# A convolution-attention and edge-branch network: 2 by 2 blocks in place of 4 by 1 columns, larger value patches, and a second layout of x

## The chip, the cores and the metric

The kernel runs on one core of a Trainium2 chip. The metric is the device time of the whole program in microseconds. Matmuls run on TensorE (PE in the profile, its weight loads PEld), elementwise work on VectorE (DVE) and ScalarE (ACT), some on GpSimd (POOL). SyncE (SP) issues nearly all DMAs; ScalarE issues those that rearrange strips and store edge features.

## The reference

The input x is (4, 512, 64, 64) in float32: four images of 512 channels. Everything is float32. The first layer is a linear attention over 64 heads of 8 channels, twice: once on q, k, v, once on their 5 by 5 depthwise and grouped pointwise convolutions.

```
q, k, v = x @ wq.T, x @ wk.T, x @ wv.T                  # over channels
pw = grouped_1x1(depthwise_5x5(concat(q, k, v)))        # 8 channels a group
f = concat(qkv, pw), in heads of 24 channels: query, key, value
query, key = relu(query), relu(key)
scores = concat(value, ones) @ key.T                    # 9 x 8 per head, over the 4096 pixels
out = scores @ query;  out = out[:8] / (out[8] + 1e-15)
y = batchnorm(proj_1x1(out)) + x
```

The second layer makes four edge maps of y (Sobel, Laplace, diagonal, gradient), multiplies each by a 128 by 512 matrix, applies batchnorm and GELU, weights the 512 results by a channel attention of their means, mixes them by a 512 by 512 matrix, normalises over channels, applies GELU and adds y.

## The kernel before

**Groups.** Each image b is cut in 4 groups of 16 heads; one `Group` object per (b, g), 16 in all. A group projects keys and values (`keys_and_values`, 8 strips of 512 pixels), then queries (`queries`). The steps of a group that use the convolved queries (`convolve(QUERY, ...)`, the second half of `correlate`, `conv_*`) are run inside the next group's `keys_and_values`. `run` and `advance` interleave the steps of the groups with the stages of the image before: `project_out`, `edge_branches`, `fuse_out`, by shares of time written out by hand (`T_CONV`, `SHARE_Y` and so on). The order of TensorE is the program's; the other engines follow the program too, each in order, and SP's DMA queue is one of them. The first image has no stage beside it. After the last group, the last image's three stages run with wider tiles (side "left"), interleaved by `fill`.

**Strips.** A strip is a half image (32 rows) and one of four row phases: rows k, k+4, k+8, ... of 64 pixels. x lies in DRAM in this order. `project` multiplies it and copies the result to `strip`; four DMAs issued by ScalarE put it into `inps[t]`, where partition = (head of four, channel, row phase), and the rows are blocks of four.

**Convolution.** `convolve` (L402) computes the depthwise and the pointwise convolution at once: for each of 5 column shifts `DXS` and 2 row blocks, a 32 by 32 matrix `mat` for each of 16 tiles of the array, 512 columns at most, summed in four PSUM banks: 160 matmuls. `load_mat` builds `mat` by one GpSimd product of the two kernels. ScalarE evicts the banks with a ReLU (L415 for keys, in the order that `correlate` needs; L421 for queries).

**Correlation.** The convolved values are never formed. `values` (L290) projects values with pixels on partitions; four DMAs a strip (L303) store them in `near`, a padded copy of the image in DRAM, split in two halves of 8 heads. `load_near` (L442) loads patches of 4 rows by 8 pixels a partition, one load for each (half, jp, b) in four DMAs: jp picks the heads, b the upper or lower row block; `vals` has 3 such buffers of 8448 bytes a partition. `correlate` (L457) multiplies transposed convolved keys by these patches, 160 columns a matmul, in two PSUM banks for each jp. `weigh` (L475, L476) multiplies by the value kernel and sums.

**Output.** `divide` and `conv_divide` write the normalised queries of the 16 heads to DRAM (`heads`, `cheads`). `project_out` loads 8 tiles of 512 pixels a strip, multiplies by the folded projection (L661), adds shift and x (L666, VectorE), and writes rows of y four apart. For the last image 16 blocks run first, since the first edge rows need all four phases of a half; then edge steps alternate with filling (`FILL_*`).

**Fusion.** `fuse_out` (L850) loads four `ef` tiles a piece (8 buffers), squares into `sq` (3 buffers) and normalises. `late` marks the last two images.

Of the kernel before, what the change touches and what calls it, by code (L numbers as in the profile page):

```python
# [8 lines left out]
F32 = mybir.dt.float32  # L9
# [35 lines left out]


NB = H // 4 + 1
# [5 lines left out]
DXS = (0, -2, -1, 1, 2)  # L53
VROW = 4 * 66
# [19 lines left out]
FILL_EACH = (16 * FILL_Y + 40 * FILL_F - FILL_FIRST - FILL_ATT) / (4 * NJ // 2 - 1)  # L74
# [3 lines left out]
T_PROJ, T_TURN, T_SCORES, T_CONV, T_CORR, T_SMALL = 3.4, 0.5, 0.3, 10.6, 1.1, 0.9  # L78


WORK, VALS = 18, 3
# [8 lines left out]
def conv_seq_kernel(  # L90
    ctx: ExitStack, tc, x, wqkv, dpk, wtab, proj, projc, pwk, bn0, consts, vec, watt1, batt1, watt2, wbr, wfuse, out
# [26 lines left out]
    def squares(ap):  # L118

        return ap.rearrange("p (b x n) -> p n x b", b=4, n=4)  # L120
# [25 lines left out]
    for t in (KEY, QUERY):  # L146
        inps[t] = keep.tile([P, 4, NB, W], F32, name=f"inp{t}")
        nc.gpsimd.memset(inps[t][:, :, 0, :], 0.0)
        nc.gpsimd.memset(inps[t][:, :, NB - 1, :], 0.0)
# [7 lines left out]
    near = [dram.tile([2, NB, W + 4, 4, 66], F32, name=f"near{n}", bufs=1) for n in range(2)]  # L157
# [3 lines left out]
    def near_border(v):  # L161

        zeros = vals.tile([P, 8 * VROW], F32, name="zeros", tag="vals")
        nc.gpsimd.memset(zeros, 0.0)
        cols = v.rearrange("a b x r d -> (a b) x (r d)")
        for at in (0, W + 2):
            nc.sync.dma_start(out=cols[:, at : at + 2, :], in_=zeros[0 : 2 * NB, 0 : 2 * VROW])
        for b, r in ((0, 0), (NB - 1, 2)):
            nc.sync.dma_start(
                out=v[:, b, :, r : r + 2, :].rearrange("a x r d -> x a (r d)"),  # L170
                in_=zeros[0 : W + 4, 0:264],
            )
# [53 lines left out]
    class Group:  # L226


        def __init__(self, b, heads, cheads, folded, g):
# [3 lines left out]
            self.strip, self.rq, self.held, self.conv, self.near = {}, {}, {}, {}, {}  # L233
            self.nears = iter([(half, jp, b) for half in range(2) for jp in range(2) for b in range(2)])
# [7 lines left out]
        def load_mat(self, t):  # L242

            dp = gw.tile([P, 4, 48], F32, name="dp_sb", tag="dp_sb", bufs=2)
            nc.sync.dma_start(out=dp, in_=dpk[self.g, t // QUERY])
            self.mat[t] = gw.tile([P, 4, 40, 8], F32, name="mat", tag="mat")
            nc.gpsimd.tensor_tensor(  # L247
                self.mat[t],
                dp[:, :, 0:40].unsqueeze(3).to_broadcast([P, 4, 40, 8]),
                dp[:, :, 40:48].unsqueeze(2).to_broadcast([P, 4, 40, 8]),  # L250
# [11 lines left out]
        def project(self, t, j):  # L262
# [12 lines left out]

            r, b = (k + 2) % 4, 8 * half + (k + 2) // 4
# [5 lines left out]
            for n in range(4):  # L282
                nc.scalar.dma_start(out=inps[t][r::4, n, b : b + 8, :], in_=rows(s)[32 * n : 32 * n + 32, :, :])

        def values(self, j):
# [14 lines left out]
            b = 8 * half + (k + 2) // 4  # L300
            for a in range(2):
                for jp in range(2):
                    nc.sync.dma_start(  # L303
                        out=self.near_dram[jp, b + a : b + a + 7 : 2, 2 : W + 2, (k + 2) % 4, :].rearrange(
                            "c x d -> x c d"
                        ),
                        in_=vt[64 * a : 64 * a + 64, :, 2 * jp : 2 * jp + 2, :].rearrange("p c q d -> p c (q d)"),
                    )
# [75 lines left out]
        def divide(self, half):  # L384
            banks = self.spread_out(self.rec)
            for k in range(4):
                j = 4 * half + k
                q = work_tile("q")
                nc.vector.tensor_mul(q, self.rq.pop(j), banks[k])
                nc.sync.dma_start(out=self.heads[j, :, self.g, :], in_=q)  # L390
# [3 lines left out]
        def convolve(self, t, half):  # L394
            banks = quad_tiles("cv")
            last = len(DXS) * 2 - 1
            for n, (dx, b) in enumerate((dx, b) for dx in DXS for b in range(2)):
# [725 lines left out]
```

## Time and profile before

Three runs took 4994.56, 5003.2 and 5009.69 us; the median is 5003.2.

| quantity | value |
|---|---|
| measured time of the profiled execution | 5007.84 us |
| its span | 5006.1 us |
| mean granted TensorE clock | 0.972 |
| VectorE busy | 2099.5 us |
| ScalarE busy | 1580.6 us |
| mean busy share of DMA engines, first queue (SP) | 52.7% |
| DMA traffic | 864.04 MB, 627,939 packets |
| packets under 512 bytes | 324,072 |
| L268 projections of keys and queries | 955.0 us, 2048 records |
| L661 output projection | 905.8 us, 2048 records |
| L290 value projections | 485.8 us, 4096 records |
| L850 fusion | 468.8 us, 1056 records |
| L738 branches | 468.9 us, 1792 records |

Busy times of matmul groups overlap a little, since each matmul's row includes the time in which the next already streams: 610 ns for a row of 512 columns, while rows start some 430 ns apart. From one start to the next is the better measure. In rows of waits the columns are: engine, operation and line, what it waited for, total us, times, longest.

### The profile page before, as it was taken

The numbers are of one execution on the slowest core, as the hardware profiler recorded it, in microseconds if no ns is written. First come the engines' busy times: TensorE is split into PE (matmuls) and PEld (weight loads), VectorE is DVE, ScalarE is ACT, GpSimd is POOL, SyncE is SP. The second block draws the span as 40 slices with busy tenths as digits, with TensorE's granted clock in tenths as the row PEclk, the third lists the DMA queues.
The fourth block names the chain that finished last, engine by engine and source line by source line (L and its number), as shares of the span: only waits on it lengthen the run. The fifth ranks groups of instructions, "written<-read, shape, count | busy, mean of one in ns | idle before, by whom it ended". The sixth has DMA issues, their size and how long they took to land. (4 is left out here: it accounts for less than half of the span.)

```text
span 5006.1 us, 106244 instructions
## 1 busy us (share of the span) xinstructions
PE 4682.3 (94%) x46140; PEld 2687.1 (54%) x46140; DVE 2099.5 (42%) x2788; ACT 1580.6 (32%) x2713; POOL 369.7 (7%) x271
## 2 busy tenths in 40 slices
PE   9999999999999999799899999989998899899897
PEld 5665654455666654354465656444446565444343
DVE  1222222114565624311356553441125565537966
ACT  2112111003454523300244443430013444304675
POOL 0000000000000012200000000220000000000343
PEclk9999999999999999899999999999999999999998
DMA  6444467675666666676556656648666565475545
GB/s 192 137 127 133 139 192 195 156 162 167 189 194 187 187 189 195 194 180 164 149 187 188 189 183 201 187 159 225 155 161 187 168 183 163 140 171 144 165 153 169
DMA packets 627939, 864.04 MB, mean 173 GB/s; under 512 B 324072, under 2 KB 381448, under 8 KB 609040
## 3 DMA queue, kind: packets, MB, share of 16 engines
q1 hardware_dynamic: 548880, 756.51, 52.7%
q10 hardware_dynamic: 78592, 100.74, 6.4%
q8 instruction: 362, 5.93, 0.5%
q14 instruction: 105, 0.86, 0.1%
HBM read 575.93 MB, written 213.98 MB: 158 GB/s over the span
## 5 line engine op out<-in xcount | busy, mean ns | idle before, releaser
L268 PE MATMUL proj<-xt,w_sb 128*128 128x512 f32 x2048 | 955.0, 610 | 55.3 <-DMA xt<-in_x 33.4
L661 PE MATMUL yps<-hd,fold_sb 128*128 128x512 f32 x2048 | 905.8, 599 | 19.5 <-DMA hd<-heads 17.4
L402 PE MATMUL cv<-inp,mat 32*32 32x512 f32 x20480 | 731.9, 597 | 40.3 <-issue 33.1
L268 PEld LDWEIGHTS proj<-xt,w_sb 128*128 128x128 f32 x2048 | 382.5, 194 | 525.5 <-issue 450.5
L661 PEld LDWEIGHTS yps<-hd,fold_sb 128*128 128x128 f32 x2048 | 386.1, 191 | 510.1 <-issue 458.2
L402 PEld LDWEIGHTS cv<-inp,mat 32*32 32x32 f32 x20480 | 422.1, 103 | 318.8 <-issue 158.2
L850 PE MATMUL zps<-ef,wf_sb 128*128 128x512 f32 (+1 forms) x1056 | 468.8, 597 | 56.5 <-DMA ef<-ef 19.0
L290 PEld LDWEIGHTS val<-w_sb,xt 128*128 128x128 f32 x4096 | 471.2, 193 | 34.5 <-issue 27.5
L290 PE MATMUL val<-w_sb,xt 128*128 128x128 f32 x4096 | 485.8, 277 | 0.6 <-DVE z L857 0.4
L738 PE MATMUL br<-maps,wbr_sb 128*128 128x256 f32 (+1 forms) x1792 | 468.9, 415 | 3.7 <-DVE s_sb L335 2.9
L666 DVE SCALAR_TENSOR_TENSOR yt<-yps,shift,xr 128x512 f32<-128x512 f32 x128 | 96.0, 750 | 837.5 <-PE yps L661 784.0
L274 ACT COPY strip<-proj 128x512 f32<-128x512 f32 x256 | 149.1, 582 | 931.0 <-PE proj L268 908.0
L738 PEld LDWEIGHTS br<-maps,wbr_sb 128*128 128x128 f32 x1792 | 338.1, 192 | 142.9 <-issue 97.1
L457 PE MATMUL corr<-near,ckt 128*32 128x160 f32 x8192 | 333.6, 315 | 35.9 <-DMA near<-near 27.5
L850 PEld LDWEIGHTS zps<-ef,wf_sb 128*128 128x128 f32 x1056 | 203.4, 196 | 299.7 <-issue 229.1
L247 POOL TENSOR_TENSOR mat<-dp_sb 128x1280 f32<-128x1280 f32 x32 | 77.5, 2421 | 3486.4 <-PE cv L402 2856.8
L457 PEld LDWEIGHTS corr<-near,ckt 128*32 128x32 f32 x8192 | 256.5, 111 | 131.9 <-issue 72.1
L714 DVE TENSOR_TENSOR maps<-dv 128x1054 f32<-128x1054 f32 (+1 forms) x112 | 158.8, 1418 | 376.5 <-PE br L738 376.3
L318 ACT ACTIVATE kt<-tr 128x512 f32<-128x512 f32 x128 | 75.8, 592 | 532.4 <-PE tr L316 350.8
L366 DVE RECIPROCAL rec<-rec 128x512 f32<-128x512 f32 x64 | 214.4, 3350 | 1.7
L746 ACT ACTIVATE ef_o<-br,shift,scale 128x256 f32<-128x256 f32 (+1 forms) x224 | 131.2, 590 | 226.8 <-PE br L738 202.8
L881 POOL TENSOR_TENSOR z<-z,yr 128x512 f32<-128x512 f32 (+1 forms) x132 | 175.9, 1351 | 293.5 <-ACT z L878 172.5
(128 smaller groups left out, 3951.8 us busy)
## 6 DMA issues: line engine op xcount, KB each, us to landing
xt<-in_x SPq DMA_DIRECT2D x316, 512.0 KB
near<-near SPq DMA_DIRECT2D x512, 264.0 KB
inp<-strip ACTq DMA_DIRECT2D x1024, 64.0 KB
win<-y SPq DMA_DIRECT2D x96, 396.0 KB
near<-vt SPq DMA_DIRECT2D x512, 66.0 KB
y<-yt SPq DMA_DIRECT2D x128, 264.0 KB
heads<-q SPq DMA_DIRECT2D x128, 256.0 KB
cheads<-cq SPq DMA_DIRECT2D x128, 256.0 KB
```

The source lines that it names most:

```text
L268: nc.tensor.matmul(ps, lhsT=self.w[t][:, c, :], rhs=xs[self.b, j][c], start=(c == 0), stop=(c == NCH - 1))
L274: nc.scalar.copy(s, ps)
L290: nc.tensor.matmul(ps[:, ts(c, P)], lhsT=xs[self.b, j][n][:, ts(c, P)], rhs=self.w[VALUE][:, n, :], start=(n == 0), stop=(n == NCH - 1),)
L366: nc.vector.reciprocal(rec, rec)
L402: nc.tensor.matmul(rows(banks[i])[32 * j : 32 * j + 32, :, c0:c1], lhsT=self.mat[t][q, j, (dx + 2) * 8 + 4 * b : (dx + 2) * 8 + 4 * b + 4, :],
L457: nc.tensor.matmul(self.banks[jj][32 * i : 32 * i + 32, 160 * b : 160 * b + 160], lhsT=self.held["c", i][:, at : at + 32], rhs=v[:, 4 * n ...
L661: nc.tensor.matmul(ps, lhsT=fold_sb[g // NG][:, g % NG, ts(c, P)], rhs=hd[g], start=(g == 0), stop=(g == 2 * NG - 1),)
L714: nc.vector.tensor_sub(flat[:, half : 3 * half - 2], dvs[:, 2 : 2 * half], dvs[:, 0 : 2 * half - 2])
L738: nc.tensor.matmul(rows(ps), lhsT=wbr_sb[:, k, c, :], rhs=rows(maps[:, slot[k], c % 2, :], WB)[:, :, 0:W], start=(c == 0), stop=(c == NCH ...
L746: nc.scalar.activation(o[:, n, :], parts[n], AF.Gelu, bias=shift1[:, k : k + 1], scale=scale1[:, k : k + 1], accum_out=pool_sb[:, k, u : u ...
L850: nc.tensor.matmul(ps, lhsT=wf_sb[:, k, ts(c, P)], rhs=ef[k], start=(k == 0), stop=(k == 3))
L881: nc.gpsimd.tensor_add(rows(z), rows(z), rows(yr, WB)[:, :, 1 : W + 1])
```

## The change

- Strips are now a half and a (row, column) phase of 2 by 2 blocks: 16 rows of 32 pixels, every second row and column. x is laid out so; `xrow`, a second copy in DRAM with rows two apart, serves the sum in `project_out`.
- `convolve` runs 9 products over block shifts (dx, dy) of -1, 0, 1; `mat` and its source have 36 columns for 40.
- `near` holds all 16 heads of a pixel together; a patch is still 4 rows by 8 pixels a partition, now with all heads, and 6 by 6 pixels of two patches surround a block of 2 by 2; one load for (half, b) in two DMAs; `vals` has 2 buffers of 16,896 bytes. `correlate` goes through jp inside b, with 192 or 96 columns a matmul, and holds two banks for each jp over both b.
- `heads` is ordered by quarter images; `project_out` walks `OUT_STRIPS` (half, quarter, row parity). `cheads` tiles are read in two DMAs. The last image runs `ALONE` = 10 blocks first.
- For room: `work` 17 buffers for 18; in the fusion of the first two images `ef` 7 for 8 and `sq` 2 for 3; `lap2` shares `win`.

```diff
-DXS = (0, -2, -1, 1, 2)
-VROW = 4 * 66
+OUT_STRIPS = [(half, u, row) for half in range(2) for u in range(2) for row in range(2)]
+BLOCKS = [(dx, dy) for dx in (0, -1, 1) for dy in (0, -1, 1)]
+PIX = 4 * 33
+PATCH = 4 * 8 * PIX
...
+ALONE = 10
...
-WORK, VALS = 18, 3
+WORK, VALS = 17, 2
...
-    near = [dram.tile([2, NB, W + 4, 4, 66], F32, name=f"near{n}", bufs=1) for n in range(2)]
+    near = [dram.tile([H + 4, W + 4, PIX], F32, name=f"near{n}", bufs=1) for n in range(2)]
...
-            for a in range(2):
-                for jp in range(2):
-                    nc.sync.dma_start(
-                        out=self.near_dram[jp, b + a : b + a + 7 : 2, 2 : W + 2, (k + 2) % 4, :].rearrange(
-                            "c x d -> x c d"
-                        ),
-                        in_=vt[64 * a : 64 * a + 64, :, 2 * jp : 2 * jp + 2, :].rearrange("p c q d -> p c (q d)"),
-                    )
+            row, col = divmod(k, 2)
+            for y in range(4):
+                at = 2 + row + 2 * y + 32 * half
+                nc.sync.dma_start(
+                    out=self.near_dram[at : at + 25 : 8, 2 + col : 2 + col + W : 2, :].rearrange("c x d -> x c d"),
+                    in_=vt[32 * y : 32 * y + 32].rearrange("p c q d -> p c (q d)"),
+                )
...
-            for n, (dx, b) in enumerate((dx, b) for dx in DXS for b in range(2)):
-                c0, c1 = _span(dx, W)
+            for n, (dx, dy) in enumerate(BLOCKS):
+                c0, c1 = _span(dx, WH)
+                at = 4 * (3 * (dx + 1) + dy + 1)
+                r0 = 1 + 16 * half + dy
...
-                            rows(banks[i])[32 * j : 32 * j + 32, :, c0:c1],
-                            lhsT=self.mat[t][q, j, (dx + 2) * 8 + 4 * b : (dx + 2) * 8 + 4 * b + 4, :],
-                            rhs=inps[t][q, j, 8 * half + b : 8 * half + b + 8, c0 + dx : c1 + dx],
+                            rows(banks[i], WH)[32 * j : 32 * j + 32, :, c0:c1],
+                            lhsT=self.mat[t][q, j, at : at + 4, :],
+                            rhs=inps[t][q, j, r0 : r0 + 16, c0 + dx : c1 + dx],
...
-                    for part in range(4):
+                    for part in range(2):
+                        v = self.near_dram[4 * (8 * half + b), 32 * part]
...
+            r0, r1 = (2 * r, 4) if b == 0 else (0, 2 + 2 * r)
+            w0 = 4 * b + r0 - 2 * r
...
-                            self.banks[jj][32 * i : 32 * i + 32, 160 * b : 160 * b + 160],
+                            self.banks[jp][jj][32 * i : 32 * i + 32, 48 * w0 : 48 * (w0 + r1 - r0)],
                             lhsT=self.held["c", i][:, at : at + 32],
-                            rhs=v[:, 4 * n : 4 * n + 20, 33 * jj + 8 * i : 33 * jj + 8 * i + 8],
+                            rhs=v[:, r0:r1, c0 : c0 + 6, 33 * (2 * jp + jj) + 8 * i : 33 * (2 * jp + jj) + 8 * i + 8],
...
-                    nc.sync.dma_start(out=xr, in_=x[b, j, :, c, :])
+                    nc.sync.dma_start(out=xr, in_=xrow[b, n, :, c, :])
...
-                        yt[:, :, 1 : W + 1], rows(ps), shift0[:, c : c + 1], rows(xr), ALU.add, ALU.add
+                        yt[:, :, 1 : W + 1].rearrange("p r (x c) -> p r x c", c=2),
+                        ps.rearrange("p (c r x) -> p r x c", c=2, r=8), shift0[:, c : c + 1],
+                        xr.rearrange("p (r x c) -> p r x c", c=2, r=8), ALU.add, ALU.add,
...
-                        t = pool.tile([P, 512], F32, name="ef", tag="ef", bufs=8)[:, :n]
+                        t = pool.tile([P, 512], F32, name="ef", tag="ef", bufs=8 if late else 7)[:, :n]
...
-    for n in range(NCH * NJ // 2):
+    for n in range(ALONE):
```

## The prediction

> **What bounds the kernel now.** I read the page's busy shares first, then its groups, then the waits of the matmul engine, and last the timeline of the stages that the change touches. All times below are of the one profiled execution: span 5006.1 us, 5007.84 us measured, which is 4.6 us above the median of the three runs, 5003.2.
>
> ```profile
> PE 4682.3 (94%) x46140; PEld 2687.1 (54%) x46140; DVE 2099.5 (42%) x2788; ACT 1580.6 (32%) x2713; POOL 369.7 (7%) x271
> PE   9999999999999999799899999989998899899897
> DVE  1222222114565624311356553441125565537966
> L402 PE MATMUL cv<-inp,mat 32*32 32x512 f32 x20480 | 731.9, 597 | 40.3 <-issue 33.1
> L457 PE MATMUL corr<-near,ckt 128*32 128x160 f32 x8192 | 333.6, 315 | 35.9 <-DMA near<-near 27.5
> ```
>
> TensorE is busy 94% of the span and above 90% in nearly every slice; its idle time is 324 us in all. VectorE comes near its limit only in the last sixth. So an instruction taken from TensorE shortens the kernel by about its own time, as long as what feeds it keeps up. The two groups the change thins are the convolution, 731.9 + 40.3 = 772 us, and the correlation, 333.6 + 35.9 = 370 us. Every matmul appears twice in the counts (64 convolutions of 160 matmuls are 10,240, and there are 20,480 records): each is two passes, with a weight load each.
>
> **Convolution, 10 products to 9.** The timeline of TensorE shows what one undisturbed convolution, one correlation step and one score step cost:
>
> ```profile
> 225.72 10.65 PE L402 MATMUL cv<-inp,mat 32*32 32x512 f32 x320
> 236.30 0.70 PE L268 MATMUL proj<-xt,w_sb 128*128 128x512 f32 x1
> ...
> 167.83 2.54 PE L457 MATMUL corr<-near,ckt 128*32 128x160 f32 x64
> 170.30 0.66 PE L316 MATMUL tr<-consts_sb,strip 128*128 128x128 f32 x4
> ...
> 180.57 0.46 PE L327 MATMUL s<-vt,kt 128*32 128x33 f32 x32
> 180.96 0.66 PE L316 MATMUL tr<-consts_sb,strip 128*128 128x128 f32 x4
> ```
>
> From start to the next start a convolution takes 236.30 - 225.72 = 10.58 us, 1.058 us a product (16 tiles, two passes). The new form has 9 products of nearly the same width: 3 of 512 columns and 6 of 496, mean 501.3, against 2 of 512, 4 of 504, 4 of 496, mean 502.4. There are 64 convolutions: 64 x 1.058 = 67.7 us. The mean granted clock is 0.972, so 67.7 / 0.972 = **70 us** come off.
>
> Here a rule speaks against the change. The Trainium skill (PSUM — Partial Sum Buffer, Specifications) says that any access pattern of a matmul that is not contiguous in PSUM slows it significantly, with 8-byte lines. The new outputs of six products are 16 rows of 31 columns, half of them from an odd column; before there were 8 rows of 62 or 63, so the breaks double. If the rule accounted for all that a product takes beyond bare streaming, about 0.22 us (1.058 less 2 x 502.4 columns at the 0.833 ns that the next paragraph's rates need), doubling the breaks would cost 64 x 6 x 0.22 = 85 us and leave almost nothing. The row decides otherwise. In the convolution above the first matmuls of the first four products start at 225.72, 226.80, 227.87 and 228.92: 1.08 us for each unbroken product and 1.05 us for the first broken one, a difference that the 2 x 16 missing columns explain (27 ns). Breaks on the reading side cost nothing either: 16 branch matmuls reading rows of 64 out of 66 take 6.86 us (4574.75 to 4581.61), and 16 output ones on whole tiles take 6.87 us (4581.61 to 4588.48). I take zero, and keep 85 us as a rival.
>
> **Correlation, 160 columns to 192 or 96.** The number of matmuls stays (4096, four at a time in the column groups), the mean width falls from 160 to 144. A step of 64 records takes 170.30 - 167.83 = 2.47 us, or 0.154 us for four; of this 160 columns at 0.833 ns are 0.133. (The rate: the 512-column rows above give 6.87 us / 16 = 0.430 us a pass, 0.84 ns a column.) At the same surplus, 192 columns are 0.181 and 96 are 0.101, mean 0.141, so 2048 groups of four save 0.0133 each: 27 us, **28 us** at the mean clock. The skill (TensorE: Matmul & The Clock Gate, Wait — 56ns, not 53.3ns?) gives a floor of about 25 ns from start to start; with it 96 columns would take 0.100 us for four, the same. But weight loads could set a higher one. The score row shows that they do not: 32 records in 0.39 us, 12 ns each. Bounds: 0 (if the short ones run no faster than 0.154 and the long ones as computed, it is even +28 us) and -28; the score row is the near one, I take -28.
>
> **Idle inside these groups.** 33.1 us of the convolution's idle time are "issue", stalls of the instruction stream; a tenth less instructions, **-4 us** with the correlation's.
>
> **Patches of values and their loads.** Per group the bytes stay: 8 loads of 128 x 8448 B before, 4 of 128 x 16896 B now. The DMAs of these loads fall from 512 to 128; those that store the values stay 512 with packets of 528 B in place of 264; reading the second half of the heads needs 256 for 128. SP issues 256 fewer, at some 0.6 us each; it does not bound. Two patches are now loaded ahead (4.3 MB) where it was three small ones (3.2 MB). These two cover the whole first half, so the waits in the middle of it go; the x strips of the last projection of a group, queued behind the second half's patches, come later.
>
> ```profile
> PE proj L268 <- DMA xt<-in_x: 33.4, 4, 18.0
> PE corr L457 <- DMA near<-near: 27.5, 7, 8.5
> PE zps L850 <- DMA ef<-ef: 19.0, 1, 19.0
> PE zps L850 <- ACT z L855: 17.2, 2, 15.0
> ```
>
> In the first row 18.0 us fall at 2088, right after such a sequence when no stage of the earlier image was left to fill in; the patch wait of 8.5 us stands 20 us before it, in the same correlation. The later patch release (a step of 2.4 us, a projection of 3.6) can make this 7 us longer; the three groups that close an image (7, 11, 15) can pay it, +21 at most. Against it stand the 27.5 us. I take **-5 us**, bounds -27 and +21.
>
> The correlation now holds four PSUM banks, but takes two at each of its first two calls, and gives them back one call apart, as before; the convolution behind it still waits for the last weighing (4.2 us in all before), which has 288 columns for 320. Nothing counted. Weights by GpSimd (2.4 us, 1152 for 1280 columns) lie beside the convolutions. ScalarE's sums of the key convolution already read columns 64 apart at 0.397 us per 256 elements, in line with 0.601 for 512 contiguous ones: nothing. The eviction of the output rows (L666, 128 at 0.750 us) now reads and writes pairs across strides. Between 0.750 and twice that: no row is near; VectorE idles 784 us waiting for these very matmuls, so outside the last stages it is covered.
>
> **Fewer buffers in the fusion of the first two images.** ef has 7 for 8: the fourth load of a piece now waits until the last channel block of the piece before has used its slot. By the instruction order, from there to its use TensorE has six passes of 0.43 us twice, 5.2 us at least, in half of the 14 cases more; a load of 256 KB in a queue that waits for it may need that or more. 0 to +20; **+5 us**. The sq buffer (2 for 3) is freed by an add of 1.5 us within 7 us of matmuls: nothing. The work tiles, 17 for 18: nothing I can point to, up to +10 in the range.
>
> **The last image.** Its edges start after 10 output blocks, not 16, because output strips now fill 16 rows at a time, and the blocks left over go between the edges.
>
> ```profile
> 4480.00:4660.00 180.00, 175.72 (x403) 76.46 (x403) 144.36 (x121) 86.05 (x75) 7.06 (x1) 0.99 0.66 171
> 4660.00:4840.00 180.00, 161.54 (x368) 70.40 (x366) 154.11 (x101) 132.79 (x165) 81.76 (x46) 0.95 0.44 142
> ```
>
> (Columns: stretch, then busy time of PE, PEld, DVE, ACT, POOL, the clock, DMA.) In these 360 us TensorE idles 22.7 us, among it the 15.0 us wait for z above, behind VectorE's edges. Six blocks of 8 x 2 passes (6 x 6.9 = 41 us) more are now there to fill. At most 22.7 us; if strided evictions cost twice, 22 of them take back 16. **-12 us.**
>
> **Sum.** -70 - 28 - 4 - 5 + 5 - 12 = -114 us. 5007.84 - 114 = **4894 us**.
>
> **Rivals.**
> 1. *The saving is given back as waits.* Three quarters of the 98 us lie in the 12 groups that are interleaved with an earlier image's stages, where ScalarE and VectorE are at half load and TensorE already idles 200 of 3125 us (1125 to 4250). If two thirds of these 73 us become waits for them, the time is 4894 + 49 = 4943. Against it: of those 200 us only some 94 are waits for these engines by name, and they keep their own work. Chance 0.15.
> 2. *Row breaks cost.* 4894 + 85 = 4979. For it the rule, against it the starts quoted. Chance 0.04.
> 3. *The patch transfers hold up x; slower.* SP works in order, and the x strips of the last query projection follow 4.3 MB of patches. Had each of the 11 other groups of images 1 to 3 the 18.0 us once seen, it were 11 x 18 = 198 us: 5092. It decides from 114 / 12 = 9.5 us a group on. For it: this wait exists and is the longest of its kind; against it: where stages of the earlier image fill in, 9.5 us of convolution and about as much of those stages again stand between, and the bytes have not grown. Chance 0.05.
>
> **How the numbers follow.** The forecast has 0.76: with its own unknowns (-22 patches, -10 last image, -5 ef; +26 x, +12, +15, and the correlation's) about 4855 to 4940. Rival 1 reaches to 4960. The range **4850 to 4950** leaves out rivals 2 and 3, the end of 1 and the far ends of the forecast. No change means within 0.3%, 15 us, about what can be told here. Faster 0.93, same 0.02 (a rival 2 with stalls), slower 0.05.
>
> **What would show it.** The convolution's group at 18,432 records and about 700 us with its idle time; one undisturbed convolution from start to next start 9.5 us (10.0 or more: breaks cost). The correlation in two shapes, some 340 us with its idle time, and no patch waits inside the first half. The longest x wait not above 25 us, and not many of them. TensorE idle in the 360 us of the last edges below 12 us. It is wrong if the convolutions shrink less than 1 us each or TensorE's idle time rises above 350 us.

## The result, and the profile after

The changed kernel takes 5287.32 us (median of four runs, 5279.85 to 5297.19); the kernel before took 5004.57 beside it (4994.56 to 5009.69). The ratio is **1.0569**, 95% interval 1.0544 to 1.0593: 5.7% slower, where the prediction had 2.3% faster. The execution whose profile follows took 5297.19 us, with a span of 5295.4.

First the page: busy shares, the line of TensorE in 40 slices, and the groups that the prediction was about.

```profile
PE 4641.1 (88%) x44092; PEld 2641.2 (50%) x44092; DVE 2084.3 (39%) x2788; ACT 1590.8 (30%) x2720; POOL 356.6 (7%) x271
PE   7999988898888889799788898879987888799987
L404 PE MATMUL cv<-inp,mat 32*32 32x512 f32 x18432 | 677.4, 605 | 63.8 <-issue 48.5
L463 PE MATMUL corr<-near,ckt 128*32 128x192 f32 (+1 forms) x8192 | 289.2, 293 | 0.0
L430 PE MATMUL ctr<-consts_sb,co 128*128 128x128 f32 x512 | 87.8, 313 | 221.3 <-ACT ckt L432 126.3
```

TensorE's share falls from 94% to 88%, though it does less. Its idle time is 5295.4 - 4641.1 = 654 us, where it was 324. Before, nearly all slices were nines; now the eights and sevens lie all over the first three images and into the last. The two groups that the change thins got thinner: convolution with its idle time 772 to 741 us, correlation 370 to 289. The largest new number stands in a group that the change does not touch, L430, the transposition of the convolved keys: 221.3 us of idle time ahead of 87.8 us of work.

The work itself shrank as computed. This is the timeline of TensorE in the first image, where one convolution and one correlation step run undisturbed:

```profile
191.30 2.25 PE L463 MATMUL corr<-near,ckt 128*32 128x192 f32 x64
193.48 0.66 PE L314 MATMUL tr<-consts_sb,strip 128*128 128x128 f32 x4
...
217.29 9.59 PE L404 MATMUL cv<-inp,mat 32*32 32x512 f32 x288
226.82 3.70 PE L268 MATMUL proj<-xt,w_sb 128*128 128x512 f32 x8
```

From start to next start the convolution takes 226.82 - 217.29 = 9.53 us (10.58 before; 9.5 was predicted), and 64 records of the correlation 193.48 - 191.30 = 2.18 us (2.47 before; 16 x 0.141 = 2.26 was predicted).

Where the time went is told by the waits of TensorE (engine, operation and line, what it waited for, total us, times, longest):

```profile
PE ctr L430 <- ACT ckt L432: 126.3, 11, 30.8
PE ctr L430 <- ACT co L417: 60.1, 4, 27.9
PE zps L860 <- DMA ef<-ef: 56.5, 9, 25.0
PE cv L404 <- issue: 48.5, 27, 4.9
PE proj L268 <- DMA xt<-in_x: 43.5, 7, 8.6
PE ctr L430 <- ACT ef_o L756: 31.3, 2, 18.4
```

The same two rows of the kernel before:

```profile
PE ctr L429 <- ACT ckt L431: 14.6, 11, 4.0
PE ctr L429 <- ACT co L415: 8.4, 3, 4.8
```

The `ef` row was 19.0. Three rows at L430 name ScalarE, in all 217.7 us; yet ScalarE is busy only 30% of the span, and its own copies (L432, 0.59 us each, as before) are as short as ever. As a wait is put down to what came last, the question is what ScalarE waited for. This is the timeline of all engines at one such wait (start, us, engine, and in brackets the idle time ahead and what ended it):

```profile
1604.26 10.67 PE L404 MATMUL cv<-inp,mat 32*32 32x512 f32 x288
1604.39 1.88 SPq L443 DMA_DIRECT2D near<-near  x2
...
1606.38 7.53 SPq L702 DMA_DIRECT2D win<-y  x1
...
1623.10 17.23 ACTq L281 DMA_DIRECT2D inp<-strip  x4
1640.38 0.64 ACT L730 ACTIVATE win<-maps 128x524 f32<-128x524 f32 x1 [16.81 <-DMA near<-near]
1640.92 0.57 ACT L432 COPY ckt<-ctr 128x512 f32<-128x512 f32 x1
...
1641.54 1.12 PE L430 MATMUL ctr<-consts_sb,co 128*128 128x128 f32 x4 [16.27 <-ACT ckt L432]
```

It is read from the end. TensorE waits 16.27 us at 1641.54 for a copy of ScalarE. ScalarE could not do it because it stood 17.23 us inside its four strip DMAs (2.6 us in the median of such quadruples). What let it go on is named by the bracket at 1640.38: the patch load `near<-near`, the second of the two in SP's row at 1604.39, issued at 1605.02, 35 us earlier. In the trace the two patch DMAs signal the completion semaphores 105 and 106 (a semaphore is a counter; a DMA raises it when its data has landed), the last times at 1630.01 and 1639.83. The third and fourth strip DMA of ScalarE use these two semaphores again and wait for them: they start at 1630.03 and 1639.85. The DMAs of SP and ScalarE take turns on eight such semaphores, whichever of the two issues them. A DMA that is long in flight so blocks the next one on its semaphore, and with it the engine that issues it. SP is held as well: its loads of x stand 97.8 us behind `near<-near`, 22.3 before. (The 7.53 us at its `win` load are not such a wait, since semaphore 107, which this load uses, was complete at 1604.73; they belong to a second path, shown under e4.)

Over the whole trace, the waits between the four strip DMAs of a quadruple sum to 366 us, 82 before. Of these, 233 us end when a patch lands on the semaphore that the next strip DMA needs; before it was 3 us.

The patch loads are long in flight. Worked out from the packets in the trace, in the median: before, 1.08 MB in four DMAs took 7.1 us from first to last packet, with 6 packets at once and 319 ns for 8448 bytes. After, 2.16 MB in two DMAs take 21.5 us, with 7 packets at once and 324 ns for only 4224 bytes. Twice the bytes take three times as long, because a packet of half the size takes the same time.

### The profile page after: what moved, and what is told of

The parts are those of the page before. It is cut to its first block, busy times and chain, and to the rows that moved or that the text cites. A ratio compares the mean times of both kernels' runs of the same rounds, so it can differ in the third digit from the quotient of the medians.

```text
span 5295.4 us, 102019 instructions
## 1 busy us (share of the span) xinstructions
PE 4641.1 (88%) x44092; PEld 2641.2 (50%) x44092; DVE 2084.3 (39%) x2788; ACT 1590.8 (30%) x2720; POOL 356.6 (7%) x271
## 3 DMA queue, kind: packets, MB, share of 16 engines
q8 instruction: 347, 5.69, 0.5%
## 5 line engine op out<-in xcount | busy, mean ns | idle before, releaser
L268 PE MATMUL proj<-xt,w_sb 128*128 128x512 f32 x2048 | 990.4, 628 | 96.4 <-DMA xt<-in_x 43.5
L404 PE MATMUL cv<-inp,mat 32*32 32x512 f32 x18432 | 677.4, 605 | 63.8 <-issue 48.5
L268 PEld LDWEIGHTS proj<-xt,w_sb 128*128 128x128 f32 x2048 | 396.4, 201 | 591.7 <-issue 474.7
L404 PEld LDWEIGHTS cv<-inp,mat 32*32 32x32 f32 x18432 | 384.6, 104 | 321.6 <-issue 162.2
L860 PE MATMUL zps<-ef,wf_sb 128*128 128x512 f32 (+1 forms) x1056 | 471.5, 599 | 83.4 <-DMA ef<-ef 56.5
L674 DVE SCALAR_TENSOR_TENSOR yt<-yps,shift,xr 128x512 f32<-128x512 f32 x128 | 95.9, 749 | 843.0 <-PE yps L669 724.1
L247 POOL TENSOR_TENSOR mat<-dp_sb 128x1152 f32<-128x1152 f32 x32 | 73.1, 2283 | 3671.2 <-PE cv L404 2981.9
L463 PE MATMUL corr<-near,ckt 128*32 128x192 f32 (+1 forms) x8192 | 289.2, 293 | 0.0
L430 PE MATMUL ctr<-consts_sb,co 128*128 128x128 f32 x512 | 87.8, 313 | 221.3 <-ACT ckt L432 126.3
L463 PEld LDWEIGHTS corr<-near,ckt 128*32 128x32 f32 x8192 | 216.9, 109 | 97.8 <-issue 46.2
L297 DVE COPY vt<-val 128x512 f32<-128x512 f32 x128 | 87.5, 683 | 290.3 <-PE val L290 273.5
```

What stands on the lines that cost most here:

```text
L268: nc.tensor.matmul(ps, lhsT=self.w[t][:, c, :], rhs=xs[self.b, j][c], start=(c == 0), stop=(c == NCH - 1))
L404: nc.tensor.matmul(rows(banks[i], WH)[32 * j : 32 * j + 32, :, c0:c1], lhsT=self.mat[t][q, j, at : at + 4, :], rhs=inps[t][q, j, r0 : r0 + ...
L430: nc.tensor.transpose(kt_ps[:, ts(c, P)], self.conv[KEY][i][:, ts(c, P)], ident)
L463: nc.tensor.matmul(self.banks[jp][jj][32 * i : 32 * i + 32, 48 * w0 : 48 * (w0 + r1 - r0)], lhsT=self.held["c", i][:, at : at + 32], rhs=v ...
L674: nc.vector.scalar_tensor_tensor(yt[:, :, 1 : W + 1].rearrange("p r (x c) -> p r x c", c=2), ps.rearrange("p (c r x) -> p r x c", c=2, r=8 ...
L860: nc.tensor.matmul(ps, lhsT=wf_sb[:, k, ts(c, P)], rhs=ef[k], start=(k == 0), stop=(k == 3))
```

## The experiments

Every ratio is to runs of the kernel before on the same chip, with its 95% interval. "Patch" is the median time from the first to the last packet of one patch; "at once" is the number of its packets in flight over that time, the mean of all patches; both are worked out from the packets in the trace. "One DMA" is the median time of one patch DMA from its issue to the last signal of its semaphore. In before and e11 a patch has half the bytes. The `cv` column and the next are waits of TensorE.

| kernel | patch loads | patch us, at once | one DMA us | `cv` issue us | L430 waits `ckt` + `co` us | clock | ratio |
|---|---|---|---|---|---|---|---|
| before | 4 x 264 KB | 7.1, 6 | 6.7 | 33.1 | 14.6 + 8.4 | 0.972 | 1 |
| after | 2 x 1056 KB | 21.5, 7 | 22.3 | 48.5 | 126.3 + 60.1 | 0.937 | 1.0569 |
| e1 | 1 x 2112 KB | 11.5, 14 | 14.3 | 137.7 | 28.4 + 33.3 | 0.963 | 1.0106 |
| e2 | 4 x 528 KB | 14.6, 9 | 8.2 | 92.0 | 31.2 + 18.7 | 0.972 | 0.9874 |
| e3 | as after, by GpSimd | 13.9, 11 | 16.2 | 140.3 | 38.2 + 31.0 | 0.959 | 1.0156 |
| e4 | as after | 21.9, 7 | 22.9 | 86.3 | 1.1 + 46.1 | 0.952 | 1.0264 |
| e7 | 8 x 264 KB | 21.4, 5 | 8.3 | 32.7 | 76.4 + 19.6 | 0.966 | 0.9985 |
| e11 | 2 x 528 KB | 5.9, 11 | 8.3 | 85.1 | 14.3 + 17.1 | 0.972 | 1.0036 |
| e12 | 4 x 528 KB | 10.5, 11 | 9.6 | 74.6 | 29.8 + 19.5 | 0.971 | 0.9860 |

**e1, e2: other shapes of the same load.** Both fill all 128 partitions with each DMA, so that the slowest dimension counts 16 and not 8; e2 also splits the patch by its four rows. In the trace 7 packets are in flight at once with 8 and 14 with 16, and a patch DMA signals its semaphore once at its issue and 8 times later in the changed kernel, 16 times in e1 and e2. This agrees with the Trainium skill (DMA: Bandwidth & Descriptors, Rules for kernel authors), which says that a slowest dimension that counts less than 16 confines a DMA to at most that many engines.

```diff
-                    for part in range(2):
-                        v = self.near_dram[4 * (8 * half + b), 32 * part]
+                    for r in range(4):
+                        v = self.near_dram[4 * (8 * half + b) + r, 0]
                         nc.sync.dma_start(
-                            out=self.near[at][64 * part : 64 * part + 64, :],
-                            in_=bass.AP(v.tensor, v.offset, [[4 * PIX, 8], [(W + 4) * PIX, 32], [1, 8 * PIX]]),
+                            out=self.near[at][:, 8 * PIX * r : 8 * PIX * (r + 1)],
+                            in_=bass.AP(v.tensor, v.offset, [[4 * PIX, 16], [4 * (W + 4) * PIX, 8], [1, 8 * PIX]]),
                         )
```

(e2; e1 has one DMA with `[[4 * PIX, 16], [(W + 4) * PIX, 32], [1, 8 * PIX]]`.)

> Edit: each patch is loaded by one DMA over all 128 partitions (outermost count 16) in place of two over 64 (outermost count 8). Theory A (slow patch transfers hold completion semaphores; ScalarE's strip DMAs take those semaphores in turn and stand in its queue, and TensorE then waits for ScalarE's evictions): the 2.16 MB of a patch used about 8 DMA engines at once and took 21.5 us from first to last packet; with 16 it takes about 11 us, ScalarE's four strip DMAs over 5 us fall from 40 to below 20, and the time falls by 130 us or more, to 5160 or less. Theory B (fewer buffers: work 17, ef 7, sq 2, and PSUM banks held longer): time within 20 us of the changed kernel's 5287, waits for ScalarE stay.

> Edit: each patch is loaded by four DMAs, one for each patch row, each over all 128 partitions (outermost count 16), 540 KB each. Theory A: the same transfer time as with one DMA, about 11 us a patch, but each completion semaphore is held for about 3 us of transfer in place of 11; ScalarE is held up less still; time at or below that of the single DMA, 5100 or less. Theory B: 5287 within 20 us.

e1: 5050.23 against 5002.01 us, ratio 1.0106 (1.0064 to 1.0148). e2: 4938.85, ratio **0.9874** (0.9859 to 0.9889). Nothing of the convolution, the correlation or the buffers differs from the changed kernel, so the loss of 5.7% lies in how the patches are loaded. The waits of TensorE in e2:

```profile
PE cv L404 <- issue: 92.0, 50, 4.3
PE ctr L430 <- ACT ckt L432: 31.2, 11, 21.5
...
PE zps L860 <- DMA ef<-ef: 6.8, 4, 3.6
```

The waits at L430 are a quarter of what they were, and the `ef` waits, 56.5 us after, are nearly gone although `ef` has its 7 buffers still. ScalarE's strip quadruples that take over 5 us fall from 40 (longest 23.7 us) to 10 (8.8 us); before there were 11. The waits of strip DMAs behind a patch fall from 233 us to 68 in e1 and 8 in e2. A patch took 14.6 us in e2, not the 11 that were expected. And a row has grown that was not expected: the convolution stalls for "issue", 92 us for 33 before.

**e3, e4: who issues.** e3 lets GpSimd issue the two patch DMAs, e4 lets GpSimd issue ScalarE's strip DMAs.

In `load_near` (e3), and for the strips at L281 (e4):

```diff
-                        nc.sync.dma_start(
+                        nc.gpsimd.dma_start(
...
-                nc.scalar.dma_start(
+                nc.gpsimd.dma_start(
```

> Edit: the patch loads, otherwise as in the changed kernel (two of 64 partitions), are issued by GpSimd in place of SyncE, and so draw completion semaphores of another set and stand in another queue. Theory A: the transfers stay as slow as they are (20 us or more), but ScalarE's strip DMAs no longer wait for them: strip issues of four over 5 us fall from 40 to 11 or so as before, TensorE's waits for ScalarE in the transposes from 217 us to below 60, time 5100 or less unless GpSimd's other work is held up. Theory C (the patches and the x behind them simply come too late for TensorE): time stays above 5230. Theory B: 5287 within 20 us.

> Edit: the strip DMAs (1024) are issued by GpSimd in place of ScalarE; patch loads as in the changed kernel. Theory A: ScalarE is never held up by a DMA semaphore; TensorE's waits for ScalarE's evictions in the transposes fall from 217 us to below 60 and the time to 5150 or less, though strips may come later to the convolutions, since GpSimd issues 1024 DMAs beside its own work. Theory C: time within 40 us of 5287. Theory B: 5287 within 20 us.

e3: 5079.85 us, ratio 1.0156 (1.0141 to 1.0171). The patches now signal semaphores of their own (111 to 118), and no strip DMA waits behind one any more. But the run was expected to keep the slow transfers, and it did not: each DMA signals 16 times, and a patch took 13.9 us with up to some 20 packets at once. So it does not separate the speed of the load from the place where it is issued. e4: 5133.47 us, ratio 1.0264 (1.0246 to 1.0282). Here the patches are as slow as in the changed kernel (21.9 us), and only ScalarE is freed:

```profile
PE zps L860 <- DMA ef<-ef: 55.8, 8, 24.4
PE yps L669 <- DMA hd<-heads: 52.1, 6, 20.4
PE ctr L430 <- ACT co L417: 46.1, 4, 23.6
...
PE ctr L430 <- ACT ckt L432: 1.1, 1, 1.1
```

The wait for L432's copies falls from 126.3 us to 1.1: taking the strip DMAs off ScalarE removes what its queue passed on, and with it about half of the loss (5.69% to 2.64%). Of what remains the largest row is the convolution's issue stall, 86.3 us; then come waits for loads of SP (`ef`, `heads`), whose queue holds the patches, and one for ScalarE, `co`, 46.1 us. This is the longest of the last kind in the timeline of e4:

```profile
3854.88 9.41 SPq L443 DMA_DIRECT2D near<-near  x4
...
3864.39 42.88 SPq L702 DMA_DIRECT2D win<-y  x3
...
3897.07 0.71 DVE L717 TENSOR_TENSOR dv<-win 128x528 f32<-128x528 f32 x1 [22.61 <-DMA win<-y]
...
3902.06 0.64 ACT L730 ACTIVATE win<-maps 128x524 f32<-128x524 f32 x1 [26.33 <-DVE maps L728]
...
3905.19 1.97 PE L430 MATMUL ctr<-consts_sb,co 128*128 128x128 f32 x8 [23.60 <-ACT co L417]
```

This is a second path, without a strip DMA in it: SP's `win` loads, which feed the edges of the image before, come behind two patches; VectorE waits for them, ScalarE, which works in order, for VectorE, and TensorE for ScalarE. The edges (L717) wait for `win` 57.3 us before, 225.2 in the changed kernel, 234.1 in e4, 82.1 in e7 and 67.4 in e2. Whether the `win` load stands in SP's queue or its packets behind the patch packets on the DMA engines, no run isolates.

**e7, e10: eight engines, small DMAs.** e7 splits the patch into eight DMAs of 264 KB with the slowest dimension 8, as in the changed kernel: the patch stays slow, the single DMA is short. e10 has besides the order of e5 below.

```diff
-                    for part in range(2):
-                        v = self.near_dram[4 * (8 * half + b), 32 * part]
+                    for r in range(8):
+                        r, part = divmod(r, 2)
+                        v = self.near_dram[4 * (8 * half + b) + r, 32 * part]
...
-                            out=self.near[at][64 * part : 64 * part + 64, :],
-                            in_=bass.AP(v.tensor, v.offset, [[4 * PIX, 8], [(W + 4) * PIX, 32], [1, 8 * PIX]]),
+                            out=self.near[at][64 * part : 64 * part + 64, 8 * PIX * r : 8 * PIX * (r + 1)],
+                            in_=bass.AP(v.tensor, v.offset, [[4 * PIX, 8], [4 * (W + 4) * PIX, 8], [1, 8 * PIX]]),
```

> Edit: the patch is cut in eight DMAs (four rows, two halves of 64 partitions, 270 KB each), each with an outermost count of 8 as in the changed kernel; the four row DMAs of 128 partitions had 16. It tells the size of a DMA from the number of engines. If the engines and so the transfer time of 21 us a patch matter (theory A with the time as its cause): about as slow as the changed kernel, 5200 or more. If the size of each DMA matters (a semaphore is held for 2.7 us of transfer): about the row-DMA run, below 5000.

e7: 4975.17 against 4979.38 us, ratio 0.9985 (0.9968 to 1.0002).

```profile
PE ctr L430 <- ACT ckt L432: 76.4, 12, 28.5
PE cv L404 <- issue: 32.7, 22, 3.4
PE zps L861 <- DMA ef<-ef: 22.3, 4, 15.3
```

A patch still takes 21.4 us, and yet the ratio is down from 1.0569 to 0.9985. So it is not how long a patch takes that cost most, but how long one DMA is in flight: 8.3 us here, 22.3 in the changed kernel. The strip DMAs wait 51 us behind patches, not 233, and the three rows at L430 are halved to 109 us; they are still above the 23 us of before. And the issue stall is back at 32.7 us: the high ones, e4's apart, belong to the loads that fill 16 engines. (A packet took 186 ns in the median here, not 324; while any is in flight there are 7 at once in both.)

**e5, e6, e8: the order in SP's queue.** The loads of patches stand ahead of the next x strips in SP's program. e5 is e2 with the loads moved behind the first convolution, and behind the second and its projection; e6 is e5 with `ALONE` back at 16; e8 is the kernel before with the same move, as far as its three buffers allow. (The lines of the schedule are shortened here.)

```diff
-                self.load_near(1)
...
-                [(0.0, lambda: self.load_near(VALS))],
...
-                cv(0), pj(2),
+                cv(0), [(0.0, lambda: self.load_near(VALS))], pj(2),
...
-                cv(1), pj(7),
+                cv(1), pj(7), [(0.0, lambda: self.load_near(VALS))],
```

> Edit: the four row DMAs a patch of the row-DMA run, and all patch loads issued behind a convolution (after the key convolution of the first half, and after that of the second half and the last query projection) in place of just ahead of them. Theory D (what is left of the loss is the instruction stream: the convolution, with most instructions a microsecond, runs dry when its instruction loads stand behind patch packets on the 16 DMA engines): the convolution's idle time marked issue falls from 92 us to 40 or less, time 4890, at most 4915. Rival E (the issue stalls belong to the new access patterns of the convolution, not to the loads): issue stays above 80 us and the time within 15 us of 4939.

> Edit: as the run with loads behind the convolutions, but 16 output blocks of the last image run ahead of its edges in place of 10. If the order of the last image is worth what the prediction took (12 us): 8 to 20 us slower than that run. Rival: the order is worth nothing, within 5 us.

> Edit: the kernel before, with its own patches, and with all patch loads issued behind the convolutions as far as its three buffers allow. If the place of the loads is what decides whatever the convolution: its issue idle in the convolution falls from 33 to below 20 us and the time by 10 to 30 us. If its small loads never did harm: within 10 us of 5002.

e5: 4926.66 against 4979.38, ratio 0.9888 (0.9867 to 0.9908). The issue stalls stay (97.0 us), as the rival that blames the convolution's access patterns had it. But the move did not do what it was for: patch packets are in flight during 46% of the convolutions' time, 47% in e2. SP runs ahead of TensorE, so a load that stands later in the program does not go out behind the convolution. The run so does not tell the two apart. e6: 0.9901 (0.9881 to 0.9921); the wait of the last stages for z comes back (17.5 us for 7.4), and the medians differ by 6 us, in the direction foreseen but inside the intervals. e8: 4937.22, ratio **0.9909** (0.9884 to 0.9934), without any of the change. Its waits:

```profile
PE cv L402 <- issue: 31.5, 24, 3.8
PE den L372 <- ACT rq L279: 28.4, 22, 7.5
PE ctr L429 <- ACT ckt L431: 26.9, 11, 6.0
PE corr L457 <- DMA near<-near: 25.4, 7, 9.2
```

The first row of before, 33.4 us for `xt`, is down to 6.2 us, and the issue stalls, expected to fall below 20 us, are as before. The x strips no longer queue behind patches. e10 shows the same for eight engines:

> Edit: the eight DMAs a patch on 8 engines of the eight-engine run, with the patch loads placed behind x loads in SyncE's program as in the run with loads behind the convolutions. Issue idle stays near 33 us (theory D: half of the engines stay free of patches), and the order of SyncE's queue gives about what it gave the kernel before, 0.9%: a ratio of 0.985 to 0.992 where the eight-engine run had 0.9985. If the order gave the kernel before its gain by another way, within 0.003 of 0.9985.

4960.63 us, ratio 0.9909 (0.9890 to 0.9928) against e7's 0.9985, as expected.

**e9: loads where nothing convolves.** e2's four DMAs, issued by ScalarE right after it has evicted the key convolution.

```diff
-                        nc.sync.dma_start(
+                        nc.scalar.dma_start(
...
-                cv(1), pj(7),
+                cv(1), [(0.0, lambda: self.load_near(VALS))], pj(7),
```

> Edit: row DMAs on 16 engines as in the row-DMA run, issued by ScalarE right behind its eviction of the key convolution of each half, so that they truly start after it (SyncE runs ahead of TensorE, and had issued them early in spite of their place in the program). Theory D (the convolution starves for instructions while patch packets fill the 16 DMA engines): issue idle in the convolution falls from 92 us to 45 or less, time 1 to 1.5% below the kernel before times 0.9874, that is a ratio of 0.975 to 0.98, unless ScalarE's own queue suffers from the 512 issues. Rival E (the new convolution's access patterns stall): issue stays above 80 us.

4934.02 against 5003.09 us, ratio 0.9853 (0.9828 to 0.9877). The ratio is above the 0.975 to 0.98 that was expected. The issue stalls are 68.5 us, between what either theory expected; patch packets are still in flight during 51% of the convolutions' time, and 60 of the 83 us of all stalls inside them fall into it. The run does not decide.

**e11: the kernel before, with 16 engines.** Each of its patches comes in two DMAs of 64 partitions whose slowest dimension counts 16, not in four of 32 partitions with 8. Bytes, convolution and correlation are those of before.

```diff
-                    for part in range(4):
-                        v = self.near_dram[jp, 8 * half + b + 4 * (part // 2), 32 * (part % 2)]
+                    for part in range(2):
+                        v = self.near_dram[jp, 8 * half + b + 4 * part, 0]
...
-                            in_=bass.AP(v.tensor, v.offset, [[4 * VROW, 8], [(W + 4) * VROW, 4], [1, 8 * VROW]]),
+                            in_=bass.AP(v.tensor, v.offset, [[4 * VROW, 16], [(W + 4) * VROW, 4], [1, 8 * VROW]]),
```

> Edit: the kernel before with each of its patches loaded by two DMAs of 64 partitions with an outermost count of 16 (540 KB each) in place of four of 32 partitions with 8. Theory D: its convolution, unchanged, now starves too: issue idle rises from 33 us to 60 or more, time 20 to 60 us above the kernel before. Rival E: issue idle within 10 us of 33, time within 15 us.

5024.34 against 5003.09 us, ratio 1.0036 (1.0023 to 1.0048). The group of the convolution:

```profile
L402 PE MATMUL cv<-inp,mat 32*32 32x512 f32 x20480 | 748.9, 607 | 90.2 <-issue 85.1
```

Before it was 731.9 busy and 33.1 us of issue. The load became only a little faster (5.9 us for 7.1): there are 11 packets at once for 6, but one takes 582 ns in the median for 319. The unchanged convolution starves 52 us more. Of the stalls inside it 55 us fall into patch packets' flight, 18 us before, though patch packets are in flight during no more of its time (35%, 38% before). So the new access patterns of the convolution are not what starves it; loads over all 16 engines are enough. The DMAs are also twice as large here, but size alone does not do it: the changed kernel, with four times the size on 8 engines, has 48.5 us.

**e12: an attempt at eight engines over all partitions.** The edit is against e2.

```diff
-                            in_=bass.AP(v.tensor, v.offset, [[4 * PIX, 16], [4 * (W + 4) * PIX, 8], [1, 8 * PIX]]),
+                            in_=bass.AP(v.tensor, v.offset, [[8 * PIX, 8], [4 * PIX, 2], [4 * (W + 4) * PIX, 8], [1, 8 * PIX]]),
```

> As e2_row_dmas (four DMAs a patch, one for each of its rows, 540 KB, 128 partitions), but the source is written as 8 pairs of positions with the pair as a second dimension, so that the slowest dimension counts 8 and each of 8 engines would write 16 neighbouring partitions instead of 8. If the half packet rate of the 64-partition loads (13 B/ns against 26.5) comes from where the partitions lie, 8 engines over 128 partitions run at about 26 B/ns: a patch takes about 2.16 MB / (8 x 26.5 B/ns) = 10 us from first to last packet, some 8 packets at once, a packet of 4224 B some 160 ns. Theory (both causes hold, ScalarE's strips behind large slow DMAs and the convolution starved by 16 busy engines): issue stalls of the convolution at or below 45 us, waits for ACT ckt L432 below 35 us, ratio to before 0.975 to 0.985, the lowest of the study. Rival (half rate comes from 8 engines or from the row length, not the partitions): a packet still about 320 ns, a patch 20 us or more, ratio 0.99 to 1.00 as with e7_eight_engines. Third case: the two outer dimensions are joined to one of 16 when the DMA is built; then about 14 packets at once, issue stalls near 92 us and a ratio of 0.987 as e2_row_dmas, and the run tells nothing new.

4925.43 against 5002.99 us, ratio 0.9860 (0.9834 to 0.9885). It is the third case: each DMA signals its semaphore 16 times, as in e2, so the two dimensions were joined. It says nothing of why packets are slow. Its issue stalls are 74.6 us, and its DMAs were issued 0.72 us apart in the median, those of e2 1.33; that explains the shorter patch, not the difference itself. The ratio cannot be told from e2's.

## Why the prediction was wrong

**The step that failed** is in the part on patches and their loads: "Per group the bytes stay: 8 loads of 128 x 8448 B before, 4 of 128 x 16896 B now. The DMAs of these loads fall from 512 to 128", with the conclusion for SP, "it does not bound", and -5 us for the whole. The loads were weighed by their bytes, by the number of their issues and by who waits for x. Four things were left out: how long one DMA of four times the size is in flight (22.3 us from issue to landing in the median, 39.7 at most, where it was 6.7 and 13.9), that other DMAs wait for its completion semaphore, that ScalarE issues such DMAs in the midst of the work that TensorE waits for, and that other loads than x, `win` above all, come behind the patches. The bound of +21 us looked only at x. Measured: strip DMAs waited 233 us behind patches for 3, the waits at L430 for `ckt`, `co` and `ef_o` alone are 217.7 us, 195 more than before, and those for `ef` grew by 37.5. VectorE's wait for `win`, the second path to L430, grew from 57.3 to 225.2 us. The paths are read from the traces, and two runs break them: without the strip DMAs on ScalarE (e4) about half of the loss goes, with short DMAs (e7) all of it, although a patch takes as long (the work that is saved still goes into waits there).

How the 289 us add up, by the two profiled executions (5007.84 and 5297.19): the idle time of TensorE grew by 330 us, its busy time fell by 41. By starts it does some 107 us less work, so the matmuls that it runs took about 66 us longer in all. The mean of L268, which the change does not touch, rose from 610 to 628 ns, 35 us over 2048 records. The mean granted clock fell from 0.972 to 0.937, and follows the loads, not the convolution: 0.952 in e4, 0.966 in e7, 0.972 in e2, which all run the changed convolution. TensorE idles 324 us before, 339 in e2, 372 in e7, 511 in e4 and 654 in the changed kernel: by and large the more, the lower the clock. That the idle stretches lower it is the likely reading; no run isolates it.

Point by point:
- **Convolution, -70.** Right: 9.53 us for 10.58, 64 x 1.05 / 0.972 = 69. The starts quoted in the prediction are not those of the products: counted by records (32 a product), the third and fourth start at 227.48 and 228.51, and the first two show 0.88 us each. Its conclusion holds all the same. In the middle of undisturbed convolutions a product of 496 columns takes 1.01 us from start to start, in 8 rows of 62 before and in 16 rows of 31 now. Row breaks cost nothing here, so the measurement stands against the sentence of the skill (PSUM — Partial Sum Buffer, Specifications) taken up in the prediction. Rival 2 falls.
- **Correlation, -28.** Right in kind, a little small: 128 x (2.47 - 2.18) / 0.972 = 38. The short matmuls ran faster than computed: where 64 of 96 columns follow each other they take 1.38 us, 0.086 for four against 0.101, so the floor that the prediction takes from the skill (TensorE: Matmul & The Clock Gate, Wait — 56ns, not 53.3ns?), 0.100 for four, did not hold for them. The patch waits inside it are gone, 27.5 to 0.
- **Issue stalls, -4.** Wrong in sign: 33.1 to 48.5 in the changed kernel, and 92.0 in e2. A tenth less instructions did not count; e11 shows that what runs beside them did.
- **x waits.** 33.4 to 43.5 us, the longest 8.6, inside what was allowed. Rival 3, the one on the slower side, had the culprit (the patch transfers) and the wrong victim: x waits are 10 us of the 289. Its price of 9.5 us a group from which it decides was passed by ScalarE's stalls, and not by x: 195 us over 12 groups are 16 us. That order costs something is real all the same: e8 gains 0.9% with it.
- **`ef` buffers, +5.** The wait rose by 37.5 us, but falls to 6.8 in e2 with the same 7 buffers: it came from the transfers.
- **Last image, -12.** From its first output block to the end 650 us before, 640 after: -10. The strided eviction (L674) takes 749 ns for 750: nothing. The difference that `ALONE` makes in e6, 6 us, is too small to be sure of.
- **Rival 1**, waits for ScalarE and VectorE in place of the saving, is what the rows show by name, at four times its size and for another reason: ScalarE was not busy, it stood in its DMA queue or waited for VectorE's maps.
- The mark set for failure, idle time above 350 us, was passed by 304.

The gain that was foreseen is partly there when the loads are kept short: the forecast was a ratio of 4894 / 5007.84 = 0.977, e2 has 0.987 and e12 0.986. The missing 1%, about 50 us, is of the size of the added issue stalls, 92.0 - 33.1 = 59 us in e2. But the order of the loads was worth a gain without the change: e8 has 0.9909 by order alone, and beside it in the same comparison e5, with the change and the same order, stands at 0.9888, with overlapping intervals. What the change adds to that kernel, 0.2%, cannot be told from nothing.

## What to carry to other kernels

Where a change merges DMAs, look at the flight time of one DMA against the time between two DMAs of any engine that shares its semaphores: an engine that also computes, and issues DMAs in between, can pass such a wait on to TensorE. A wait "for ScalarE" at low ScalarE load is followed further back, into its DMA queue and to what its own work waited for, before anything is planned for ScalarE. How many DMA engines a load fills is a trade: 16 cost the convolution 59 us of stalls more in e2, 8 left 86 us more of waits at L430 in e7. No run here has both low.

## What the hardware showed that was not expected

- A DMA of ScalarE waits for a DMA of SP that it has nothing to do with, 17.23 us in the case shown. Of 256 strip quadruples 40 took over 5 us in the changed kernel, and 11 before; the excess over 2.5 us is 375 us and 105.
- Loads that use all 16 engines starve the convolution: 33.1 to 85.1 us of issue stalls in e11, where only the patch loads changed. In the kernels where SP or ScalarE issue patches and strips, these stalls are 31 to 49 us with patch loads on 8 engines and 68 to 138 with 16; with DMAs issued by GpSimd they were 86 (e4) and 140 (e3). In the trace the instructions themselves come as DMA packets on a queue of their own (347 of 16 KB). Of the 40 stalls over 1 us inside e2's convolutions, 31 end 1.3 to 1.7 us after such a packet has ended; of all convolution matmuls 7% start so. The packets do not take longer (1.09 us in the median of e2, 1.05 before). That they start late, behind patch packets on the same engines, fits, and is not isolated.
- A packet of 4224 bytes took as long (324 ns in the median, 13.0 bytes per ns) as one of 8448 before (319 ns, 26.5). In e1, over 128 partitions and 16 engines, it is 13.0 as well; in e11, over 64 partitions with 4 neighbours to an engine, 14.5; in e7, with the engines and partitions of the changed kernel, 22.7. The Trainium skill (SBUF — State Buffer, Door 1: The DMA port swizzle) says that 64 partitions reach no more ports than 32; that would leave the rate as it was, and does not halve it. An estimate from the table of ports there: two engines share a port in the changed kernel, e1 and e11, and each has its own in the kernel before. That fits these four rates, but not e7, where they would share too. It stays open.
